# A graph layer on one Trainium2 core: grouped node sums from three bfloat16 parts instead of one float32 product

## The chip, the cores and the metric

The kernel runs on one core of one Trainium2 chip. The metric is the device time of one execution in microseconds (us). A core has a matrix engine (TensorE, shown as PE, with its weight loads shown apart as PEld), a vector engine (VectorE, DVE), a scalar engine (ScalarE, ACT), a general engine (GpSimd, POOL) and a queue for transfers (SyncE, SP). Each engine executes its own instructions in the order of the program, and the engines wait for one another by semaphores. Matmuls write to PSUM, which has eight banks here, split by the kernel into four with the tag "A" and four with the tag "B".

## The reference, cut to what matters

There are 6250 nodes with 128 features and 200,000 edges; `dst` is sorted, `src` is random. One layer computes

```python
h = relu(layernorm(x)); xw = h @ W_in                       # per node
W_ij = (shifted_softplus(f_ij @ W_f1 + b_f1) @ W_f2 + b_f2) * f_ij_cutoff   # per edge
x_ij = xw[idx_j] * W_ij
out  = segment_sum(x_ij, idx_i, num_segments=6250)          # idx_i = src, unsorted
y = x + shifted_softplus(out @ W_o1 + b_o1) @ W_o2 + b_o2
```

`idx_i` is `src` and `idx_j` is `dst`, so the gather follows the sorted index and the sum goes to random nodes. The sum over edges is the part that the change touches.

## The kernel before, in words

The edges are cut into 391 blocks of 512. `Plan` puts them in a list of 411 items, and one loop walks over it with a software pipeline: step `i` does the first stage of item `i`, the second of item `i-1` and so on. There are three kinds of items.

- **S items** (231): the product of an edge's filter and its gathered node row (`m`) goes through a matmul with an equality matrix (`s3_pe`, tile `pp`), is copied out by ScalarE (`s3_copy`, tile `s`), and is added to one of four accumulators in memory by four scatter transfers of 128 rows, issued by GpSimd (`scatter`, L491). Five buffers hold `s`.
- **B items** (160): the block's edges are first permuted by a matmul with a one-hot matrix (`perm_oh` makes it, `permute` writes the tiles `pf` and `po`, `perm_out` copies them out on ScalarE as `bfe` and `vf`), so that each edge lies in one of 512 places belonging to 16 groups of 392 nodes, 32 places each. Edges that find no place go to an overflow part, `po`. `b_ext` then multiplies by a small selection matrix to get each place's cutoff and its local node number; the result lies in 12 columns of the same bank as `po`, and `b_ext_copy` brings it to SBUF as `ex`. The product of filter and node row stays in SBUF as `bm`.
- **V items** (20): the overflow of eight B items, handled as an S item.

Eight B items are a **round**, 20 in all. When a round's eight products are there, four **units** sum them into `accT`, which holds all nodes in SBUF. Unit `s` of a round does for each of the eight blocks: a one-hot tile `so` of 128 places by 392 nodes, with the cutoff multiplied in (`unit_oh`, L671), and then per group of 32 places a matmul of the product by that one-hot tile (`unit_pe`, L686), 32 matmuls into four banks "B", one for each group. Being float32, each is two passes, so the profile counts 64. `unit_evac` (L694, L696) adds the four banks to `accT`.

The order of work is fixed by hand. Each step has named points, in order "L", "D0", the stages themselves, "A0", "A1", "DM", "PE2", "A2", "D2", and `at(step, point, function)` hangs work on them. A unit at step k has `unit_oh` at "D2" of step k-1, `unit_pe` at "PE2" of step k and `unit_evac` at "D1" of step k+1. A permutation planned for step u has `permute` at "PE2" of u, `perm_out` at "A0" of u+1, `b_ext` at "PE2" of u+1 and `b_ext_copy` at "D0" of u+2. `b_copy` brings a B item's gathered rows from PSUM to SBUF at "A0" of its own step.

The tiles with the tag "B" take the four banks in turn. A unit takes all four, so it waits for the readers of the four tiles that were taken before it. Most units come in pairs, at steps k and k+2 (32 times); the next one after a pair, or after a single unit, comes five or more steps later.

Plan lays a unit where the item two steps before is a B and the item after is an S. The products of B items, the index loads at the start and the loads of `x` for the tail share one pool `bp` of 16 buffers of 2 KB per partition.

After the loop, a tail sums the accumulators and `accT`, and computes the output layers.

Of the kernel before, what the change touches and what calls it, by code (L numbers as in the profile page):

```python
# [20 lines left out]
P = 128  # L21
# [29 lines left out]
def tile_gnn(ctx: ExitStack, tc: tile.TileContext, x, fS, fN, cT, srcT, srcr, dstr, dstT, base0, win_, wf1, wfB, wf2,  # L51
# [17 lines left out]
    NG = len(groups)  # L69
    XEARLY = min(8, len(tgroups))  # L70
    pl = Plan(NQ)
# [19 lines left out]
    dp = ctx.enter_context(tc.tile_pool(name="dp", bufs=1, space=DRAM))  # L91
    bp = ctx.enter_context(tc.tile_pool(name="bp", bufs=pl.nbm))
    edge = ctx.enter_context(ExitStack())
# [36 lines left out]
    iotw = cp.tile([P, GN // 2 + SLOTS], F16, name="iot")  # L130
    iot = iotw[:, GN // 2:]
    tri = cp.tile([P, P], BF16, name="tri")
    onesb = cp.tile([P, P], BF16, name="onesb")
# [278 lines left out]

    def b_copy(n):
        xc = wk.tile([P, 4, P], F32, tag="xc", name="xc")
        nc.scalar.copy(xc, bq[pl.items[n][1]].pop("xg"))
        st[n]["xc"] = xc

    def s2_m(n):
        kind, q = pl.items[n]
        if kind == "B":  # L420
            m = bp.tile([P, 4, P], F32, tag="bm", name="bm")
            bq[q]["m"] = m
        else:
            m = ms[pl.sd[n] % 2]
        nc.vector.tensor_tensor(m[:, :, :P], st[n]["W"], st[n]["xc"], op=ALU.mult)  # L425
        st[n]["m"] = m
        if kind == "B":
            del st[n]
# [198 lines left out]
    def perm_out(q):  # L627
        r, j = divmod(pl.bo[q], RND)
        f = wk.tile([P, 512], BF16, tag="bf", name="bfe", bufs=pl.nf)
        nc.scalar.copy(f[:KS], bq[q].pop("pf")[:KS])  # L630
        bq[q]["f"] = f
        if j == 0:
            vq[r] = {"f": wk.tile([P, 512], BF16, tag="vf", name="vf")}
        nc.scalar.copy(vq[r]["f"][:KS, j * OVC:(j + 1) * OVC], bq[q]["po"][:KS, :OVC])

# [4 lines left out]
    def b_ext(q):  # L640
        slot_ext(bq[q]["po"][:, OVC:OVC + 12], bq[q]["f"])

    def b_ext_copy(q):
        ex = wk.tile([P, 4, 3], F32, tag="ex", name="ex", bufs=pl.nex)
        nc.vector.tensor_copy(ex.rearrange("p c k -> p (c k)"), bq[q].pop("po")[:, OVC:OVC + 12])  # L645
        bq[q]["ex"] = ex
# [17 lines left out]

    so_t = {}

    def unit_oh(r, s):
        for q in pl.rounds[r]:
            so = wk.tile([P, GN], F32, tag="so", name="so", bufs=SOB)
            ex = bq[q]["ex"]  # L670
            nc.vector.tensor_scalar(so, iotw[:, :GN], ex[:, s, 1:2], ex[:, s, 0:1], op0=ALU.is_equal, op1=ALU.mult)  # L671
            so_t[q] = so

    un = {}

    def unit_pe(r, s):
        ts = []
# [3 lines left out]
        qs = pl.rounds[r]  # L681
        for q in qs:
            so = so_t.pop(q)
            for g in range(4):
                v = slice(g * CAP, (g + 1) * CAP)
                nc.tensor.matmul(ts[g][:, :GN], bq[q]["m"][v, s, :], so[v], start=(q == qs[0]), stop=(q == qs[-1]))  # L686
        un[r, s] = ts
# [22 lines left out]
    def x_load(g):  # L710
        o, T = tgroups[g]
        xts[g] = bp.tile([P, 4, P], F32, tag="bm", name="xb")
        nc.sync.dma_start(xts[g][:, :T], x[o:o + T * P, :].rearrange("(t p) f -> p t f", p=P))  # L713

    def load_idx(s, lo, hi):
        dst_sb = bp.tile([HALF, hi - lo], I32, tag="bm", name="dst_sb")
        nc.sync.dma_start(dst_sb, dstr[s * HALF:(s + 1) * HALF, lo:hi])
        src_i = bp.tile([HALF, hi - lo], I32, tag="bm", name="src_i")
        nc.sync.dma_start(src_i, srcr[s * HALF:(s + 1) * HALF, lo:hi])
        idx[s, lo] = (dst_sb, src_i)  # L720
# [7 lines left out]
    def src_cols(a, b):  # L728
        t_ = bp.tile([P, b - a], I32, tag="bm", name="srci")
        nc.sync.dma_start(t_, srcT[:, a:b])  # L730
        late["srci"] = t_
# [4 lines left out]
    def src_cast(s, lo, hi, eng):  # L736
        s16 = bp.tile([HALF, hi - lo], I16, tag="bm", name="s16")
        eng.tensor_copy(s16, idx[s, lo][1])
        nc.sync.dma_start(src16[s * HALF:(s + 1) * HALF, lo:hi], s16)

    with tc.manual_schedule():
# [56 lines left out]
        def rel(s, lo, hi):  # L798
            dst_sb = idx[s, lo][0]
            k0, k1 = lo // WSEG, hi // WSEG  # L800
            b_ = base_i[:, s, k0:k1]
            nc.vector.tensor_scalar(b_, dst_sb[:, ::WSEG], con[:HALF, 5 + s:6 + s], 0.0, op0=ALU.min, op1=ALU.max)
            rel_f = bp.tile([HALF, hi - lo], F32, tag="bm", name="rel_f")
# [3 lines left out]
            rel_b = bp.tile([HALF, hi - lo], BF16, tag="bm", name="rel_b")  # L807
# [56 lines left out]
        def at(i, point, fn, *a):  # L864
            hooks.setdefault((i, point), []).append((fn, a))
# [112 lines left out]
        for r, qs in enumerate(pl.rounds):  # L978
# [14 lines left out]
            for q in qs:  # L993
# [13 lines left out]
        for k, (r, s) in pl.units.items():  # L1007
# [3 lines left out]

        banked = {prep_tp: 1, prep_mm: 1, rank_count: 1, rank_over: 1, permute: 2, v_ext: 1, v_row: 1, late_bias: 1,
                  r0_tp: 1}
# [245 lines left out]
class Plan:  # L1259
    def __init__(self, nq):  # L1260
# [29 lines left out]
        for r, qs in enumerate(self.rounds):  # L1290
            i = max(self.pos[qs[-1]] + 2, done + 1)
            nxt = self.pos[self.rounds[r + 1][-1]] + 2 if r + 1 < len(self.rounds) else 0
            free = [k for k in range(i, nxt) if kind(k - 2) in ("B", "") and kind(k + 1) == "S" and kind(k) != "V"]
            rest = [k for k in range(max(free[-1:] + [i - 1]) + 1, i + 40) if "V" not in (kind(k), kind(k + 1))]
# [10 lines left out]
        self.perm, prev = {}, 0  # L1305
        for q in bs:
# [8 lines left out]
        self.nbm = 16  # L1315
        self.nf = 5
# [130 lines left out]
```

## Time and profile before

| | |
|---|---|
| three runs | 2489.48, 2496.16, 2496.21 us, median 2496.16 |
| the profiled execution | 2483.28 us |
| its span, first to last instruction | 2481.5 us |
| mean granted TensorE clock | 0.914 |
| busy: PE, DVE, ACT, POOL | 2074.5, 1723.3, 1528.0, 1648.4 us |
| units' matmuls (L686), busy | 621.1 us |
| units' one-hot tiles (L671), busy | 274.7 us |

Busy time is the union of an engine's instructions. A row of a group ends with the busy time, the mean of one instruction in ns, and the idle time of the engine just before those instructions, by what ended it. A wait between engines is given as the total, the number of times and the longest. In the timeline a row is a start, a length, the engine, the line and the instruction with its count, and in brackets the idle time before it and who ended it.

### The profile page before, as it was taken

To read this page: it belongs to the slowest core of one execution; us is meant where nothing else is said; L and a number is where in the kernel's file an instruction comes from. 1 tells how busy PE (TensorE), PEld (TensorE's weight loads), DVE (VectorE), ACT (ScalarE), POOL (GpSimd) and SP (SyncE) were. 2 spreads that over 40 slices of the span, in tenths; PEclk is the share of its full clock that TensorE was granted. 3 is DMA by queue.
4 is the path that set the end of the run, shared out by engine and by line. 5 is a ranking of instruction groups with operands and counts; after the bars stand their busy time and mean duration, and the time that the engine had idled before them with its cause. 6 is when DMAs were issued, how large, how long until landed. Compare 5 with 4: busy or idle time off the path is not lost. (4 is left out here: it accounts for less than half of the span.)

```text
span 2481.5 us, 50737 instructions
## 1 busy us (share of the span) xinstructions
PE 2074.5 (84%) x17477; PEld 1440.0 (58%) x17477; DVE 1723.3 (69%) x4345; ACT 1528.0 (62%) x3733; POOL 1648.4 (66%) x1060
## 2 busy tenths in 40 slices
PE   1678897988998898888889898989898897989955
PEld 1466665655665565655566565656566565656633
DVE  4666767677786767776776758677676766676744
ACT  1677565557575666656575765757576675667524
POOL 3578866748575667657585857677576776668674
PEclk8787898999998999989999999999999998999978
DMA  6766544536363455445464545455454554545748
GB/s 204 185 134 98 91 74 76 102 47 109 60 117 59 78 86 99 74 71 92 83 95 84 84 60 92 75 96 84 67 84 67 97 80 82 77 67 86 146 54 226
DMA packets 422469, 232.17 MB, mean 94 GB/s; under 512 B 156823, under 2 KB 399690, under 8 KB 422210
## 3 DMA queue, kind: packets, MB, share of 16 engines
q0 software_dynamic: 146032, 72.35, 28.7%
q1 hardware_dynamic: 275746, 156.49, 24.2%
q8 instruction: 138, 2.26, 0.4%
q14 instruction: 121, 0.99, 0.1%
q10 hardware_dynamic: 432, 0.08, 0.0%
HBM read 126.43 MB, written 102.32 MB: 92 GB/s over the span
## 5 line engine op out<-in xcount | busy, mean ns | idle before, releaser
L491 POOL DMA_INDIRECT acc<-s,ji x1003 | 1598.7, 1594 | 780.3 <-ACT ji L472 446.8
L686 PE MATMUL un<-so,bm 32*128 32x392 f32 x5120 | 621.1, 578 | 177.8 <-DVE ex L645 143.6
L447 ACT COPY s<-pp 128x258 f32<-128x258 f32 x502 | 172.8, 379 | 668.0 <-PE pp L439 485.4
L686 PEld LDWEIGHTS un<-so,bm 32*128 32x128 f32 x5120 | 332.0, 220 | 431.6 <-DVE ex L645 181.6
L401 PE MATMUL W<-w,a 128*128 128x128 f32 x3288 | 489.9, 293 | 3.5 <-DVE a L368 2.7
L401 PEld LDWEIGHTS W<-w,a 128*128 128x128 f32 x3288 | 410.2, 196 | 72.0 <-issue 32.1
L696 DVE TENSOR_TENSOR accT<-un,accT 128x392 f32<-128x392 f32 x304 | 150.8, 558 | 317.1 <-PE un L686 277.8
L368 DVE SCALAR_TENSOR_TENSOR a<-z,e 128x512 f32<-128x512 f32 x411 | 281.1, 684 | 110.3 <-ACT e L336 92.0
L439 PE MATMUL pp<-m,eq 128*128 128x129 f32 x2008 | 297.4, 291 | 12.4 <-DVE rt L601 4.9
L336 ACT ACTIVATE e<-e,con 128x512 f32<-128x512 f32 x411 | 296.7, 722 | 13.4
L439 PEld LDWEIGHTS pp<-m,eq 128*128 128x128 f32 x2008 | 267.5, 198 | 43.1 <-ACT s L447 6.5
L425 DVE TENSOR_TENSOR m<-W,xc 128x512 f32<-128x512 f32 x251 | 172.5, 687 | 168.9 <-ACT xc L410 148.4
L410 ACT ACTIVATE xc<-xg,cb 128x128 f32<-128x128 f32 x924 | 264.5, 380 | 25.3 <-PE xg L389 25.3
L330 ACT ACTIVATE e<-z 128x512 f32<-128x512 f32 x411 | 254.0, 618 | 39.5 <-PE z L315 21.9
L671 DVE TENSOR_SCALAR so<-iot,ex 128x392 f32<-128x392 f16 x640 | 274.7, 499 | 2.9 <-PE un L686 2.6
L331 ACT ACTIVATE e<-e 128x512 f32<-128x512 f32 x411 | 258.9, 630 | 13.1
L612 DVE TENSOR_SCALAR pm<-iot,pos 128x576 bf16<-128x576 f16 x640 | 205.3, 383 | 10.2 <-issue 6.8
L623 PE MATMUL pf<-pm,st 128*108 128x512 bf16 x640 | 203.5, 412 | 6.6 <-DVE ex L645 3.3
L384 PE MATMUL W<-b2rep,onesb 64*128 64x512 bf16 x411 | 161.9, 394 | 10.3 <-ACT xc L410 5.9
L307 PE MATMUL xgb<-wb,bfe 42*128 42x128 bf16 x1920 | 163.8, 220 | 0.0
L359 DVE TENSOR_TENSOR eq<-sb,srcT_sb 128x512 f32<-128x512 int16 x231 | 157.4, 682 | 1.3 <-issue 1.3
L304 PE MATMUL z<-bfe,wsb 64*128 64x512 bf16 (+2 forms) x480 | 152.0, 388 | 0.0
(171 smaller groups left out, 2217.1 us busy)
## 6 DMA issues: line engine op xcount, KB each, us to landing
sb<-src SPq DMA_DIRECT2D x231, 128.0 KB
acc<-s,ji POOLq DMA_INDIRECT x1003
rb<-reld SPq DMA_DIRECT2D x231, 64.0 KB
fsd<-f SPq DMA_DIRECT2D x29, 480.0 KB
ft<-fsd SPq DMA_DIRECT2D x115, 120.0 KB
fb<-in_fS_dram SPq DMA_DIRECT2D x29, 320.0 KB
ta_in<-acc SPq DMA_DIRECT2D x36, 256.0 KB
ft<-fsd SPq DMA_DIRECT2D x115, 80.0 KB
```

Of the source, the lines that this page charges most:

```text
L330: nc.scalar.activation(e, st[q]["z"], AF.Abs)
L331: nc.scalar.activation(e, e, AF.Exp, scale=-1.0)
L336: nc.scalar.activation(e, e, AF.Ln, bias=half, scale=0.5)
L368: nc.vector.scalar_tensor_tensor(a, st[q]["z"], 0.0, st[q]["l"], op0=ALU.max, op1=ALU.add)
L401: nc.tensor.matmul(W[:, c, :], st[n]["a"][:, c * P:(c + 1) * P], w2, start=False, stop=(c == 3))
L410: nc.scalar.mul(xc[:, c, :], st[n]["xg"][:, c, :], v)
L439: nc.tensor.matmul(pp[:, c, :129], st[n]["eq"][:, k, :], m[:, k, :129], start=True, stop=True)
L491: nc.gpsimd.indirect_dma_start(out=accs[k][:, :], out_offset=bass.IndirectOffsetOnAxis(ap=ji, axis=0), in_=s, in_offset=None, compute_op=A ...
L612: nc.vector.tensor_scalar(pm[:, c], iot[:, :SLOTS], rk[r]["pos"][:, 4 * j + c:4 * j + c + 1], None, op0=ALU.is_equal)
L623: nc.tensor.matmul(f[:KS], w, pm[:, c, :GRP * CAP], start=(c == 0), stop=(c == 3))
L671: nc.vector.tensor_scalar(so, iotw[:, :GN], ex[:, s, 1:2], ex[:, s, 0:1], op0=ALU.is_equal, op1=ALU.mult)
L686: nc.tensor.matmul(ts[g][:, :GN], bq[q]["m"][v, s, :], so[v], start=(q == qs[0]), stop=(q == qs[-1]))
```

## The change

The unit's matmuls become bfloat16. `unit_oh` splits the eight blocks' products for unit `s` into three bfloat16 parts: the high half of each float32 word, read in place as every second bfloat16 element (`high`), then the remainder's high half, then the rest (`low`). The one-hot tiles become bfloat16 and no longer carry the cutoff. `unit_pe` runs 96 single-pass matmuls, three per block and group, where it ran 64 passes. The cutoff is multiplied in earlier: `b_copy` becomes four ScalarE multiplications of 128 columns by `ex`, instead of one copy of 512.

`b_ext` now writes to a bank of its own, `be`, so `po` is done with when `perm_out` has copied it. `Plan.ext` puts `b_ext` at the first step after the permutation that is not a unit's; `b_ext_copy` follows one step later. The products lie in two fixed arrays of eight blocks, used by even and odd rounds, instead of the pool of 16, and the early temporaries and the loads of `x` use slices of them. Units have to lie two steps apart, which moves the last round's four from steps 405, 406, 407, 408 to 406, 408, 410, 412; all others stay. Ten permutations move later, by one or two steps.

```diff
@@ b_copy
-        nc.scalar.copy(xc, bq[pl.items[n][1]].pop("xg"))
+        xg = bq[q].pop("xg")
+        for c in range(4):
+            nc.scalar.mul(xc[:, c, :], xg[:, c, :], bq[q]["ex"][:, c, 0:1])
@@ s2_m
-            m = bp.tile([P, 4, P], F32, tag="bm", name="bm")
-            bq[q]["m"] = m
+            r, j = divmod(pl.bo[q], RND)
+            m = bms[r % 2][:, j]
@@ b_ext, b_ext_copy
-        slot_ext(bq[q]["po"][:, OVC:OVC + 12], bq[q]["f"])
+        t = ps.tile([P, 512], F32, tag="B", name="be", bufs=4)
+        slot_ext(t[:, :12], bq[q]["f"])
+        bq[q]["te"] = t
...
-        nc.vector.tensor_copy(ex.rearrange("p c k -> p (c k)"), bq[q].pop("po")[:, OVC:OVC + 12])
+        nc.vector.tensor_copy(ex.rearrange("p c k -> p (c k)"), bq[q].pop("te")[:, :12])
@@ unit_oh, unit_pe
+    def high(t):
+        return t.bitcast(BF16)[:, :, 1::2]
...
-        for q in pl.rounds[r]:
-            so = wk.tile([P, GN], F32, tag="so", name="so", bufs=SOB)
-            ex = bq[q]["ex"]
-            nc.vector.tensor_scalar(so, iotw[:, :GN], ex[:, s, 1:2], ex[:, s, 0:1], op0=ALU.is_equal, op1=ALU.mult)
+        m = bms[r % 2][:, :, s]
+        rm = wk.tile([P, RND, P], F32, tag="rem", name="rem", bufs=1)
+        nc.vector.tensor_tensor(rm, m, high(m), op=ALU.subtract)
+        lo = wk.tile([P, RND, P], BF16, tag="low", name="low", bufs=1)
+        nc.vector.tensor_tensor(lo, rm, high(rm), op=ALU.subtract)
+        for q in qs:
+            so = wk.tile([P, GN], BF16, tag="so", name="so", bufs=SOB)
+            nc.vector.tensor_scalar(so, iotw[:, :GN], bq[q]["ex"][:, s, 1:2], None, op0=ALU.is_equal)
...
-        for q in qs:
-            so = so_t.pop(q)
-            for g in range(4):
-                v = slice(g * CAP, (g + 1) * CAP)
-                nc.tensor.matmul(ts[g][:, :GN], bq[q]["m"][v, s, :], so[v], start=(q == qs[0]), stop=(q == qs[-1]))
+        for j in range(RND):
+            for k in range(3):
+                for g in range(4):
+                    v = slice(g * CAP, (g + 1) * CAP)
+                    nc.tensor.matmul(ts[g][:, :GN], parts[k][v, j, :], sos[j][v],
+                                     start=(j == 0 and k == 0), stop=(j == RND - 1 and k == 2))
@@ the schedule
-                at(u + 1, "PE2", b_ext, q)
-                at(u + 2, "D0", b_ext_copy, q)
+                at(pl.ext[q], "PE2", b_ext, q)
+                at(pl.ext[q] + 1, "D0", b_ext_copy, q)
@@ Plan
-            i = max(self.pos[qs[-1]] + 2, done + 1)
+            i = max(self.pos[qs[-1]] + 2, done + 2)
+            self.ext[q] = next(e for e in range(u + 1, p - 1) if e not in self.units)
+            load[self.ext[q]] = load.get(self.ext[q], 0) + 1
```

More of the change, by code (lines that the diff above doesn't have):

```diff
@@ L69, in tile_gnn @@
     NG = len(groups)
-    XEARLY = min(8, len(tgroups))
+    XEARLY = min(RND, len(tgroups))
     pl = Plan(NQ)
@@ L131, in tile_gnn, with tmp @@
     iot = iotw[:, GN // 2:]
+    bms = []
+    for i in range(2):
+        bm_ = cp.tile([P, RND, 4, P], F32, name=f"bm{i}")
+        bms.append(bm_)
+    tmp_n = [0]
+    def tmp(rows, n, dt):
+        k = tmp_n[0] % (2 * RND)
+        tmp_n[0] += 1
+        v = bms[k // RND][:rows, k % RND].rearrange("p s f -> p (s f)")
+        return v[:, :n] if dt == F32 else v.bitcast(dt)[:, :n]
     tri = cp.tile([P, P], BF16, name="tri")
@@ L413, in b_copy @@
     def b_copy(n):
+        q = pl.items[n][1]
         xc = wk.tile([P, 4, P], F32, tag="xc", name="xc")
-        nc.scalar.copy(xc, bq[pl.items[n][1]].pop("xg"))
+        xg = bq[q].pop("xg")
+        for c in range(4):
+            nc.scalar.mul(xc[:, c, :], xg[:, c, :], bq[q]["ex"][:, c, 0:1])
         st[n]["xc"] = xc
@@ L633, in perm_out @@
             vq[r] = {"f": wk.tile([P, 512], BF16, tag="vf", name="vf")}
-        nc.scalar.copy(vq[r]["f"][:KS, j * OVC:(j + 1) * OVC], bq[q]["po"][:KS, :OVC])
+        nc.scalar.copy(vq[r]["f"][:KS, j * OVC:(j + 1) * OVC], bq[q].pop("po")[:KS, :OVC])
     def slot_ext(t, f):
@@ L663, in v_row @@
         vq[r]["row"] = t
-    so_t = {}
+    def high(t):
+        return t.bitcast(BF16)[:, :, 1::2]
+    un = {}
     def unit_oh(r, s):
-        for q in pl.rounds[r]:
-            so = wk.tile([P, GN], F32, tag="so", name="so", bufs=SOB)
-            ex = bq[q]["ex"]
-            nc.vector.tensor_scalar(so, iotw[:, :GN], ex[:, s, 1:2], ex[:, s, 0:1], op0=ALU.is_equal, op1=ALU.mult)
-            so_t[q] = so
-    un = {}
+        qs = pl.rounds[r]
+        m = bms[r % 2][:, :, s]
[3 more added lines that the diff above has]
+        nc.vector.tensor_tensor(lo, rm, high(rm), op=ALU.subtract)
+        sos = []
+        for q in qs:
+            so = wk.tile([P, GN], BF16, tag="so", name="so", bufs=SOB)
+            nc.vector.tensor_scalar(so, iotw[:, :GN], bq[q]["ex"][:, s, 1:2], None, op0=ALU.is_equal)
+            sos.append(so)
+        un[r, s] = (high(m), high(rm), lo), sos
     def unit_pe(r, s):
+        parts, sos = un.pop((r, s))
         ts = []
@@ L1290, in __init__ @@
         for r, qs in enumerate(self.rounds):
-            i = max(self.pos[qs[-1]] + 2, done + 1)
+            i = max(self.pos[qs[-1]] + 2, done + 2)
             nxt = self.pos[self.rounds[r + 1][-1]] + 2 if r + 1 < len(self.rounds) else 0
             free = [k for k in range(i, nxt) if kind(k - 2) in ("B", "") and kind(k + 1) == "S" and kind(k) != "V"]
-            rest = [k for k in range(max(free[-1:] + [i - 1]) + 1, i + 40) if "V" not in (kind(k), kind(k + 1))]
+            rest = [k for k in range(max(free[-1:] + [i - 2]) + 2, i + 40, 2) if "V" not in (kind(k), kind(k + 1))]
             free = (free + rest)[:4]
@@ L1314, in __init__ @@
         self.nwin = 14
-        self.nbm = 16
         self.nf = 5
```

20 lines of the change are left out of this document (9 added, 11 removed).

## The prediction, made before the changed kernel ran

> **What bounds the kernel now.** I read the page's busy shares, then the waits, then the timeline around one pair of units. The page and its groups:
>
> ```profile
> span 2481.5 us, 50737 instructions
> ...
> PE 2074.5 (84%) x17477; PEld 1440.0 (58%) x17477; DVE 1723.3 (69%) x4345; ACT 1528.0 (62%) x3733; POOL 1648.4 (66%) x1060
> ...
> L491 POOL DMA_INDIRECT acc<-s,ji x1003 | 1598.7, 1594 | 780.3 <-ACT ji L472 446.8
> ...
> L686 PE MATMUL un<-so,bm 32*128 32x392 f32 x5120 | 621.1, 578 | 177.8 <-DVE ex L645 143.6
> ...
> L671 DVE TENSOR_SCALAR so<-iot,ex 128x392 f32<-128x392 f16 x640 | 274.7, 499 | 2.9 <-PE un L686 2.6
> ```
>
> The waits (total, times, longest):
>
> ```profile
> ACT s L447 <- PE pp L439: 485.4, 78, 14.2
> POOL acc L491 <- ACT ji L472: 446.8, 92, 36.2
> DVE accT L696 <- PE un L686: 277.8, 64, 7.6
> POOL acc L491 <- issue: 245.9, 805, 0.6
> ...
> DVE m L425 <- ACT xc L410: 148.4, 131, 19.2
> PE un L686 <- DVE ex L645: 143.6, 57, 6.2
> ...
> ACT s L447 <- DMA acc<-s,ji: 87.6, 19, 11.4
> ```
>
> No engine is full. The other engines wait for PE, and they do it at the units: ScalarE waits 485.4 us for matmuls that stand behind a unit, VectorE 277.8 us for the units' banks, and the scatter queue in turn 446.8 us for ScalarE. PE's own wait inside a unit is for `ex`. The chain that ended last is only the tail, so the timeline must show the price. A pair of units, steps 316 and 318, first VectorE, then PE, then ScalarE:
>
> ```profile
> 1859.90 3.23 DVE L671 TENSOR_SCALAR so<-iot,ex 128x392 f32<-128x392 f16 x8
> 1863.05 0.17 DVE L645 COPY ex<-po 128x12 f32<-128x12 f32 x1
> ...
> 1868.19 1.98 DVE L696 TENSOR_TENSOR accT<-un,accT 128x392 f32<-128x392 f32 x4 [1.74 <-PE un L686]
> ...
> 1871.29 3.23 DVE L671 TENSOR_SCALAR so<-iot,ex 128x392 f32<-128x392 f16 x8
> ...
> 1877.70 1.20 DVE L612 TENSOR_SCALAR pm<-iot,pos 128x576 bf16<-128x576 f16 x4
> 1878.82 0.16 DVE L645 COPY ex<-po 128x12 f32<-128x12 f32 x1
> ...
> 1885.60 1.99 DVE L696 TENSOR_TENSOR accT<-un,accT 128x392 f32<-128x392 f32 x4 [6.35 <-PE un L686]
> ...
> 1863.27 5.53 PE L686 MATMUL un<-so,bm 32*128 32x392 f32 x58 [1.68 <-DVE ex L645]
> ...
> 1875.94 0.24 PE L638 MATMUL po<-selb,bfe 108*128 108x3 bf16 x4 [0.77 <-ACT vf L634]
> 1876.11 0.93 PE L686 MATMUL un<-so,bm 32*128 32x392 f32 x6
> 1879.04 7.16 PE L686 MATMUL un<-so,bm 32*128 32x392 f32 x58 [2.00 <-DVE ex L645]
> ...
> 1875.66 0.22 ACT L634 CAST vf<-po 108x64 bf16<-108x64 f32 x1
> ```
>
> Both units stop after six passes, at the fourth bank, until an `ex` copy ends. The two are of different kinds. At the first, that copy stands directly behind the unit's own one-hot tiles: VectorE, without a gap, sets the start (1863.22, PE goes on at 1863.27). At the second, the fourth bank is the `po` permuted one step earlier. Its `ex` copy is planned for "D0" of the step after the unit, behind `pm`, so PE waits to 1879.04 though the tiles were ready at 1874.52. PE then runs slow (7.16 against 5.53 us), and VectorE, done at 1885.60 - 6.35 = 1879.25, idles 6.35 us.
>
> From the plan and the order in which the banks are taken, 37 of the 80 units have a permutation one step before (second kind), 38 are of the first kind, and five end the loop.
>
> **The change part by part.** *The second kind.* `po` is now free when ScalarE has copied `vf`. That copy moves later by the new `b_copy`, which stands before it at "A0":
>
> ```profile
> L415 ACT COPY xc<-xgb 128x512 f32<-128x512 f32 x160 | 92.2, 577 | 0.0
> ...
> L410 ACT ACTIVATE xc<-xg,cb 128x128 f32<-128x128 f32 x924 | 264.5, 380 | 25.3 <-PE xg L389 25.3
> ```
>
> One copy took 0.577 us; four multiplications take 264.5/231 = 1.145 us, so +0.57 us. The unit's length: each of 96 passes needs a weight load, and the row for four loads of 128 bfloat16 columns, beside rows for float32 loads and for a permutation's matmuls, is the first of these:
>
> ```profile
> 1875.83 0.26 PEld L638 LDWEIGHTS <-bfe 108*128 108x128 bf16 x4 [1.05 <-ACT bfe L630]
> ...
> 1879.85 0.35 PEld L686 LDWEIGHTS un<-so,bm 32*128 32x128 f32 x4 [0.30 <-issue]
> ...
> 1281.09 4.90 PEld L686 LDWEIGHTS un<-so,bm 32*128 32x128 f32 x58 [0.87 <-DVE ex L645]
> ...
> L638 PEld LDWEIGHTS <-bfe 108*128 108x128 bf16 x640 | 36.2, 97 | 58.2 <-ACT bfe L630 46.9 <-issue 4.6 <-ACT e L336 1.0
> ...
> 1217.37 0.40 PE L623 MATMUL pf<-pm,st 128*108 128x512 bf16 x1
> ...
> 1217.64 0.40 PE L623 MATMUL pf<-pm,st 128*108 128x512 bf16 x1
> ```
>
> (0.26 - 0.097)/3 = 0.054 us a load, 5.2 us a unit. The low end lets loads hide: a pass streams 576 columns (512 and po's 64) in 0.27 us, so 392 in 0.18, and four row groups run at once: 24 x 0.18 = 4.4 us. The high end takes the float32 load, (4.90 - 0.18)/57 = 0.083 us: 8.0 us. I take 5.2, since the loads have that row's width and type.
>
> [...] No row here shows a stepped load.
>
> At step 318 the unit ends at 1875.88 + 0.57 + 0.05 + 5.2 = 1881.7 instead of 1886.20: 4.5 us. VectorE must have finished its own work to profit; that slides by its extra 1.0 us (below), so at most 6.35 - 1.0 = 5.35 us comes through. The smaller of the two, unit by unit over the 37, sums to **199 us** (5.4 each; 188 to 207 for 1.5 and 0.6 us extra). First and last:
>
> ```profile
> 267.20 7.54 PE L686 MATMUL un<-so,bm 32*128 32x392 f32 x58 [4.37 <-DVE ex L645]
> ...
> 274.13 1.99 DVE L694 COPY accT<-un 128x392 f32<-128x392 f32 x4 [6.73 <-PE un L686]
> ...
> 2272.62 8.34 PE L686 MATMUL un<-so,bm 32*128 32x392 f32 x58 [2.21 <-DVE ex L645]
> ...
> 2280.35 1.98 DVE L696 TENSOR_TENSOR accT<-un,accT 128x392 f32<-128x392 f32 x4 [7.52 <-PE un L686]
> ```
>
> *VectorE's extra work.* Two subtractions over 8 x 128 elements. The neighbours:
>
> ```profile
> L254 DVE TENSOR_TENSOR fr<-fb,f 128x640 f32<-128x640 f32 x29 | 23.7, 817 | 0.0
> ...
> 1207.33 0.42 DVE L222 TENSOR_TENSOR rm<-xps,x 128x256 f32<-128x256 f32 x1
> ```
>
> 0.397 us for 384 elements more is 1.03 ns each, so 1.21 us for 1024, 2.4 for both. Eight bfloat16 tiles: `pm` does 576 columns in 1.20/4 = 0.30 us, the same operation with the same types; 392 columns lie between 0.20 (in proportion) and 0.30, and I take 0.25: 2.0 us. Together 4.4 against 274.7/80 = 3.4: **+1.0 us** a unit, ends +0.6 and +1.4.
>
> *The first kind.* The fourth bank is now mostly `be`, whose `ex` copy again stands directly behind `unit_oh`. These 38 units start 1.0 us later and take 5.2 instead of 5.53: +0.7. PE's wait grows from 1.68 to 2.7 us. The pair shows a slow unit after 2.00 us of waiting; I add 0.4, since some of the 38 are slow already (ends 0 and 1.5, the excess of 7.16 over 5.53 in proportion). 38 x 1.1 = **-42 us**, ends +20 (a unit of 4.4 us, +0.6) and -98.
>
> [...]
>
> *ScalarE.* 160 x 0.57 = 91 us. Six of a round's eight B items stand around units, where ScalarE idles for `pp` (485.4 us) and the `vf` part is already counted. Two stand between, where VectorE waits on ScalarE (148.4 us for `xc`): 40 x 0.57 = **-23 us**, ends 0 and -91. If the idle time goes, all 91 are paid.
>
> *The rest.* `ex` copies stay 160; `be` adds one bank taken per B item, but `po` leaves earlier, so I cost it at nothing; what covers it is the VectorE order, and without that a wait of `pp` for an `ex` copy is next. The last units spaced by two let the scatter queue fill: **+6 us**, ends 0 and 10. Fixed arrays keep the rotation of 16 products; nothing. The scatters do not change: 1003 x 1.594 + 245.9 = 1845 us, below the forecast. DMAs and SP's queue keep their number and place, except as steps move.
>
> Sum: 199 - 42 - 23 + 6 = 140 us. Against the profiled execution's 2483.28 that is 2343; the median of the runs, 2496.16, lies 12.9 us above it, so **2356 us**.
>
> **The rivals.**
>
> *Stepped weight loads cost like float32* (slower). A unit takes 8.0 us. On PE's side alone the second kind saves 5.9 us on average (4.5 at step 318), now 5.9 - 2.8 = 3.1, or 115 us, which VectorE no longer limits; the first loses 1.0 + 2.5 + 0.4 = 3.9, or 148; ScalarE 23, the last five 4: 2483 + 60, or about 2556 with the same offset. It decides from 7.3 us a unit, 0.076 a load. For it: no stepped load is in the trace. Against: a float32 load reads every byte that a stepped one spans, and in the row of four the next loads follow at (0.35 - 0.18)/3 = 0.055 us, as the bfloat16 loads do.
>
> *VectorE and ScalarE take all of it* (no change). All ends at once: 188 - 98 - 91 = -1, so 2497. For it: VectorE then has no gap between a pair's units. Against: three ends must meet.
>
> *The scatter queue gives part back.* The 87.6 us in which ScalarE waits for a free `s` grow when PE is sooner. If half the gain goes there, 2426. Against: the queue starves 446.8 us, and starvation is what shrinks.
>
> *More comes out.* The low unit length, no ScalarE cost: 207 + 20 + 6 = 233, so 2263.
>
> **How the numbers follow.** Forecast (2310 to 2410) 0.56; scatter queue 0.15; more 0.11; no change 0.08, of which 0.05 within bounds and 0.03 slower; stepped loads 0.10. Faster: 0.56 + 0.15 + 0.11 = 0.82. Three runs spread by 0.3%, which is what a measurement can tell. The range 2265 to 2475 leaves out the no-change and stepped-load cases above, 0.18, and the edge of the case below.
>
> **What would show it.** Right: L686's successor shows no wait on `ex` at the second kind but one on `vf` of about 1.3 us, 5.2 us from its fourth bank to its end, and its busy time falls from 621.1 to some 430; VectorE's wait for `un` falls from 277.8 to under 120; the scatter queue's for `ji` from 446.8 to about 310; the first kind still waits for `ex`, longer. Wrong: weight loads spaced over 0.07 us, or waits of PE on the new `low` and `so` tiles.

## The result, and the profile after

The changed kernel takes **2306.96 us** (median of four runs, 2301.08 to 2313.85) against 2495.05 (2489.48 to 2496.21), a ratio of 0.9251 with a 95% interval of 0.9222 to 0.9281. Profiled execution against profiled execution it is 2307.47 against 2483.28: **176 us less**, where the sum of the prediction gave 140; by the medians it is 188. The time lies inside the range of 2265 to 2475, 49 us below the point.

In this kernel's profile the unit's matmul is L709, its one-hot tiles L695, the two subtractions L689 and L691, the multiplied `b_copy` L428, `ex`'s copy L660, the sum into `accT` L720, `b_ext`'s matmuls L651. From its page:

```profile
span 2305.3 us, 56334 instructions
PE 1915.0 (83%) x20037; PEld 1376.3 (60%) x20037; DVE 1793.0 (78%) x4505; ACT 1613.1 (70%) x4213; POOL 1675.5 (73%) x1060
```

From its groups by line:

```profile
L504 POOL DMA_INDIRECT acc<-s,ji x1003 | 1625.8, 1621 | 576.5 <-ACT ji L485 249.9 <-issue 233.2 <-DMA acc<-s,ji 52.2
L709 PE MATMUL un<-so,bm 32*128 32x392 bf16 x2560 | 378.7, 377 | 181.5 <-DVE so L695 79.9 <-DVE ex L660 43.1 <-ACT xc L428 22.3
L695 DVE TENSOR_SCALAR so<-iot,ex 128x392 bf16<-128x392 f16 x640 | 162.0, 326 | 0.0
L691 DVE TENSOR_TENSOR low<-rem 128x1024 bf16<-128x1024 f32 x80 | 98.0, 1225 | 2.7
L689 DVE TENSOR_TENSOR rem<-bm 128x1024 f32<-128x1024 f32 x80 | 97.5, 1219 | 0.0
L428 ACT ACTIVATE xc<-xgb,ex 128x128 f32<-128x128 f32 x640 | 181.8, 370 | 0.0
L651 PE MATMUL be<-selb,bfe 108*128 108x3 bf16 x640 | 39.8, 166 | 8.9 <-ACT bfe L643 7.1 <-DVE rt L614 0.7 <-issue 0.4
```

From its waits (total, times, longest):

```profile
POOL acc L504 <- ACT ji L485: 249.9, 76, 35.7
ACT s L460 <- PE pp L452: 238.8, 65, 8.0
DVE accT L720 <- PE un L709: 138.7, 60, 5.5
PEld L709 <- DVE so L695: 126.9, 75, 4.9
PE un L709 <- DVE so L695: 79.9, 43, 4.5
ACT s L460 <- DMA acc<-s,ji: 76.7, 18, 8.4
PE un L709 <- DVE ex L660: 43.1, 31, 1.7
```

The three large waits of before have halved or nearly: ScalarE for `pp` 485.4 to 238.8, the scatter queue for `ji` 446.8 to 249.9, VectorE for the units' banks 277.8 to 138.7. What has grown is PE's wait for one-hot tiles, from 18.7 us to 79.9 (its weight loads, which come first, show 126.9). The wait for `ex` inside a unit has fallen from 143.6 to 43.1 and no longer occurs at the second kind.

The same pair of units as in the prediction, steps 316 (first kind) and 318 (second), in the timeline; first VectorE, then PE:

```profile
1716.73 1.23 DVE L691 TENSOR_TENSOR low<-rem 128x1024 bf16<-128x1024 f32 x1
...
1717.87 1.98 DVE L695 TENSOR_SCALAR so<-iot,ex 128x392 bf16<-128x392 f16 x8
1719.78 0.16 DVE L660 COPY ex<-be 128x12 f32<-128x12 f32 x1
...
1725.51 1.99 DVE L720 TENSOR_TENSOR accT<-un,accT 128x392 f32<-128x392 f32 x4 [2.53 <-PE un L709]
...
1728.61 1.22 DVE L689 TENSOR_TENSOR rem<-bm 128x1024 f32<-128x1024 f32 x1
1729.86 1.22 DVE L691 TENSOR_TENSOR low<-rem 128x1024 bf16<-128x1024 f32 x1
1731.00 1.94 DVE L695 TENSOR_SCALAR so<-iot,ex 128x392 bf16<-128x392 f16 x8
...
1737.88 1.99 DVE L720 TENSOR_TENSOR accT<-un,accT 128x392 f32<-128x392 f32 x4 [1.48 <-PE un L709]
...
1718.24 0.34 PE L709 MATMUL un<-so,bm 32*128 32x392 bf16 x3 [1.95 <-DVE so L695]
...
1719.99 0.48 PE L709 MATMUL un<-so,bm 32*128 32x392 bf16 x1 [1.40 <-DVE ex L660]
...
1720.29 0.83 PE L709 MATMUL un<-so,low 32*128 32x392 bf16 x4
...
1720.62 0.83 PE L709 MATMUL un<-so,bm 32*128 32x392 bf16 x4
...
1723.18 0.48 PE L709 MATMUL un<-so,bm 32*128 32x392 bf16 x4
...
1723.35 0.48 PE L709 MATMUL un<-so,rem 32*128 32x392 bf16 x4
...
1731.78 0.34 PE L709 MATMUL un<-so,bm 32*128 32x392 bf16 x1
1732.58 0.32 PE L709 MATMUL un<-so,bm 32*128 32x392 bf16 x1 [0.46 <-ACT xc L428]
1733.06 0.43 PE L709 MATMUL un<-so,bm 32*128 32x392 bf16 x2 [0.15 <-ACT bfe L643]
1733.18 0.48 PE L709 MATMUL un<-so,rem 32*128 32x392 bf16 x4
...
1736.84 0.47 PE L709 MATMUL un<-so,low 32*128 32x392 bf16 x4
```

At step 318 the unit stops for 0.46 and 0.15 us in ScalarE's order (`b_copy`, then `bfe` and `vf`), and from 1733.06 it runs through: four passes each 0.166 us, 22 such rows in the 3.66 us from 1733.18 to 1736.84. VectorE idles 1.48 us before it, where it idled 6.35. At step 316 PE waits 1.95 us for the first one-hot tile, does three passes, stops 1.40 us at the fourth bank for the `ex` copy behind the eighth tile, and then needs 0.33 us for four passes until about 1722.3, and 0.17 after. The granted clock is 1.00 up to the first passes there and 0.50 from 1720 to 1722.3.

All 80 units, sorted by the kind that they had in the kernel before (37 of the second kind, 38 of the first, and the five that end the loop). The numbers are means per unit, worked out from each unit's rows; "PE" is the wait before its first pass plus the time from there to the end of its last:

| kind | PE, before | PE, after | wait before the first pass | wait for `ex` inside | VectorE idle before `accT` |
|---|---|---|---|---|---|
| second (37) | 11.94 | 6.12 | 0.00 to 0.64 | 3.33 to 0.00 | 6.67 to 0.56 |
| first (38) | 8.36 | 9.49 | 0.44 to 1.88 | 0.54 to 1.13 | 2.18 to 2.62 |
| last five | 7.90 | 8.68 | 0.41 to 0.92 | 0.00 to 0.00 | 1.42 to 4.44 |

That is 37 x 5.82 = 215 us gained, 38 x 1.13 = 43 lost and 5 x 0.78 = 4 lost: 168 of the 176. The other 8 are a gain and a loss elsewhere. The gain is at `b_ext`'s matmuls. The group of before, not shown in the prediction:

```profile
L638 PE MATMUL po<-selb,bfe 108*128 108x3 bf16 x640 | 39.4, 166 | 35.1 <-ACT vf L634 34.3 <-issue 0.8
```

Before, they stood one step behind the permutation, directly ahead of a unit where that step had one, and PE idled 35.1 us, nearly all for ScalarE's copies of the permuted tiles; now, at a step without a unit, 8.9: 26 us gained in this accounting, which goes by PE's time; no run moves `b_ext` alone. What is left, 176 - 168 - 26 = -18 us, is the loss in all other places.

### The profile page after: what moved, and what is told of

The parts are those of the page before. It is cut to its first block, busy times and chain, and to the rows that moved or that the text cites. A ratio compares the mean times of both kernels' runs of the same rounds, so it can differ in the third digit from the quotient of the medians.

```text
span 2305.3 us, 56334 instructions
## 1 busy us (share of the span) xinstructions
PE 1915.0 (83%) x20037; PEld 1376.3 (60%) x20037; DVE 1793.0 (78%) x4505; ACT 1613.1 (70%) x4213; POOL 1675.5 (73%) x1060
## 3 DMA queue, kind: packets, MB, share of 16 engines
q14 instruction: 125, 1.02, 0.1%
## 4 chain that ended last, share of the span: by engine, by line
DVE 27%; PE 26%; ACT 20%; issue 8%; DMA 7%; POOL 6%; SPq 5%; ACTq 0%; DVEq 0%; POOLq 0%
PE un L709 14%; DMA acc<-s,ji 6%; POOL acc L504 5%; DVE so L695 4%; PE W L411 4%; ACT xc L420 4%; ACT xc L428 3%; ACT e L341 3%; DVE a L378 3%; ACT e L340 3%; PE pp L452 3%; DVE accT L720 3%; DVE rem L689 3%; ACT s L460 2%; DVE bm L438 2%
## 5 line engine op out<-in xcount | busy, mean ns | idle before, releaser
L504 POOL DMA_INDIRECT acc<-s,ji x1003 | 1625.8, 1621 | 576.5 <-ACT ji L485 249.9
L709 PE MATMUL un<-so,bm 32*128 32x392 bf16 x2560 | 378.7, 377 | 181.5 <-DVE so L695 79.9
L460 ACT COPY s<-pp 128x258 f32<-128x258 f32 x502 | 172.0, 385 | 365.8 <-PE pp L452 238.8
L709 PE MATMUL un<-so,rem 32*128 32x392 bf16 x2560 | 352.4, 379 | 0.0
L709 PE MATMUL un<-so,low 32*128 32x392 bf16 x2560 | 349.3, 375 | 0.0
L452 PEld LDWEIGHTS pp<-m,eq 128*128 128x128 f32 x2008 | 265.3, 197 | 64.0 <-ACT s L460 12.9
L720 DVE TENSOR_TENSOR accT<-un,accT 128x392 f32<-128x392 f32 x304 | 150.8, 558 | 139.8 <-PE un L709 138.7
L709 PEld LDWEIGHTS <-bm 32*128 32x128 bf16 x2560 | 139.0, 106 | 196.3 <-DVE so L695 126.9
L709 PEld LDWEIGHTS <-rem 32*128 32x128 bf16 x2560 | 132.7, 106 | 115.4 <-issue 81.8
L428 ACT ACTIVATE xc<-xgb,ex 128x128 f32<-128x128 f32 x640 | 181.8, 370 | 0.0
```

Of the source, the lines that this page charges most:

```text
L428: nc.scalar.mul(xc[:, c, :], xg[:, c, :], bq[q]["ex"][:, c, 0:1])
L452: nc.tensor.matmul(pp[:, c, :129], st[n]["eq"][:, k, :], m[:, k, :129], start=True, stop=True)
L504: nc.gpsimd.indirect_dma_start(out=accs[k][:, :], out_offset=bass.IndirectOffsetOnAxis(ap=ji, axis=0), in_=s, in_offset=None, compute_op=A ...
L709: nc.tensor.matmul(ts[g][:, :GN], parts[k][v, j, :], sos[j][v], start=(j == 0 and k == 0), stop=(j == RND - 1 and k == 2))
L720: nc.vector.tensor_tensor(v, t[:, :GN], v, op=ALU.add)
```

## The experiments

Each is a version of one of the two kernels. Ratios are to the kernel before, which was measured again beside each group of versions, with medians of 2490.49, 2492.68 and 2494.95 us. A difference of some 5 us between versions of different groups therefore says little.

| version | median us (range) | ratio [95%] |
|---|---|---|
| before, bank alone | 2248.86 (2247.14 to 2250.91) | 0.9031 [0.9014, 0.9049] |
| after, bank undone | 2539.59 (2537.51 to 2543.51) | 1.0200 [1.0179, 1.0222] |
| after, cutoff left out | 2251.76 (2243.55 to 2256.61) | 0.9044 [0.9013, 0.9074] |
| after, no subtractions | 2153.88 (2149.64 to 2161.14) | 0.8655 [0.8629, 0.8681] |
| the same, one part | 2113.97 (2109.22 to 2118.63) | 0.8466 [0.8445, 0.8488] |
| before, bank and cutoff | 2268.60 (2266.32 to 2271.37) | 0.9092 [0.9070, 0.9115] |
| after, early `ex` | 2241.59 (2236.60 to 2243.88) | 0.8978 [0.8954, 0.9002] |
| before, bank and early `ex` | **2198.12** (2195.90 to 2204.27) | 0.8818 [0.8795, 0.8842] |
| after, tiles first | 2304.08 (2299.28 to 2310.32) | 0.9235 [0.9216, 0.9254] |
| after, early `ex`, tiles first | 2217.71 (2212.99 to 2222.51) | 0.8901 [0.8884, 0.8919] |
| after, early `ex`, cutoff left out | 2203.84 (2199.48 to 2208.43) | 0.8838 [0.8817, 0.8859] |

**Which part of the change gains?** The theory was the prediction's: the bank does, and the split alone loses or breaks even. The rival was that cheaper matmuls carry it. First the bank and its schedule alone, with float32 units:

```diff
-        slot_ext(bq[q]["po"][:, OVC:OVC + 12], bq[q]["f"])
+        t = ps.tile([P, 512], F32, tag="B", name="be", bufs=4)
+        slot_ext(t[:, :12], bq[q]["f"])
...
-                at(u + 1, "PE2", b_ext, q)
-                at(u + 2, "D0", b_ext_copy, q)
+                at(pl.ext[q], "PE2", b_ext, q)
+                at(pl.ext[q] + 1, "D0", b_ext_copy, q)
...
```

> The kernel before, with the bank part alone: the product for cutoff and place gets a bank of its own at the new steps, and the units stay float32 with the cutoff in the one-hot tiles. Theory of the prediction (the wait for the ex copy at the fourth bank is the gain): the 37 units of the second kind start when ScalarE has copied vf, without the 0.57 us of the new multiplications, and take 5.5 us; each saves about 6.0 us, the first kind is as before, so 222 us less than 2495, about 2275 (2255 to 2305), which would be faster than the whole change. Rival (the shorter bfloat16 unit is the gain): at most 60 us less, 2435 or more.

Then the changed kernel with this part undone:

> The changed kernel, with the bank part undone: the product for cutoff and place goes back into po's bank at the old steps, and the units stay three bfloat16 parts, the cutoff on ScalarE. Theory: the second kind still waits for the late ex copy, 1.0 us later than before, and is 1.5 us shorter (18 us saved), the first kind starts 1.0 us later and is about 1.4 us shorter (15 us saved), ScalarE costs 23: within 25 us of before, 2470 to 2520. Rival (the shorter unit is the gain): 2400 or less.

Measured 2248.86 and 2539.59. The waits of the bank alone (the unit's matmul is L688 there), and then its groups by line:

```profile
ACT s L447 <- PE pp L439: 265.3, 62, 8.3
DVE accT L698 <- PE un L688: 101.9, 47, 4.7
PE un L688 <- DVE ex L647: 14.9, 16, 1.8
```

```profile
L688 PE MATMUL un<-so,bm 32*128 32x392 f32 x5120 | 560.5, 525 | 48.0 <-DVE so L673 16.5 <-DVE ex L647 14.9 <-issue 5.7
...
L638 PE MATMUL be<-selb,bfe 108*128 108x3 bf16 x640 | 39.8, 166 | 6.5 <-ACT bfe L630 4.7 <-DVE ra L600 0.6 <-issue 0.6
```

The same two views of the kernel with the bank undone:

```profile
PE un L707 <- DVE ex L658: 202.8, 70, 7.1
DVE accT L718 <- PE un L707: 327.5, 74, 6.8
```

```profile
L651 PE MATMUL po<-selb,bfe 108*128 108x3 bf16 x640 | 39.4, 166 | 62.6 <-ACT vf L647 58.7 <-ACT xc L428 2.6 <-ACT bfe L643 1.3
```

The bank gains 246 us without the split (2495 to 2249, or 242 against the kernel before of its own group) and 233 with it (2540 to 2307); the split loses 45 without the bank and 58 with it. So the bank is more than the whole gain. The same float32 unit that took 11.94 us takes 6.36 at the second kind when nothing stops it. Of these 5.6 us, 3.5 are waits, and 2.1 are busy time (8.45 to 6.36): before, the mean granted clock inside these units was 0.78, and below 0.9 in 36 of the 37; with the bank alone it is 1.00 in all of them. Weighted by the granted clock the busy time hardly changes (6.50 to 6.36), so the slow clock after the stop is this second part of the price. The run lies below the theory's range, which began at 2255: beside the units, `b_ext`'s own wait fell from 35.1 us to 6.5. The part as a whole was tested; no run separates the bank of its own from the moved step of `b_ext` and the ten moved permutations.

With the bank undone the units wait 202.8 us in all for `ex`, 158 of them at the second kind, where it was 123 before, since `ex` now stands behind more VectorE work. And `b_ext` waits 62.6 us for ScalarE where it waited 35.1, since the four multiplications stand ahead of the copies that it reads. The theory's range ended at 2520; this second loss was not in it.

**What does the cutoff cost?** First it is taken out of the changed kernel, by the edit below. Then the multiplications are put into the version with the bank and float32 units, by the reverse of this edit; the one-hot tiles there no longer multiply by the cutoff.

```diff
-        for c in range(4):
-            nc.scalar.mul(xc[:, c, :], xg[:, c, :], bq[q]["ex"][:, c, 0:1])
+        nc.scalar.copy(xc, xg)
```

> The changed kernel, with one ScalarE copy of 512 columns in place of the four multiplications; the cutoff is left out for the blocks of the grouped sums. Theory: the multiplications cost 23 us, so 2284 (2275 to 2300). Rival (ScalarE sets the stretches between the units): all 91 us come back, 2216.

> The bank part alone, and the cutoff multiplied on ScalarE as in the change, the units still float32 (one-hot tiles without the cutoff, 64 passes). Theory (ScalarE's 91 us come through by the 55 that leaving them out gave): 2249 + 55 = 2304, or up to 20 less if the one-hot tile with one operation is quicker than 0.43 us: 2280 to 2310. It would put nearly the whole loss of the split against the bank alone on ScalarE. Rival (the subtractions, +1.0 us of VectorE a unit, are the loss): 2249 to 2265.

Measured: 55 us less (2307 to 2252), and 20 us more (2249 to 2269). A third run, below, gives 38. ScalarE's work is the same each time, 181.8 us in the changed kernel against 92.2 before, so in the changed kernel and its version with the early copy two to three fifths of the 90 us come through. The 20 us of the float32 version is a net figure: its one-hot tiles became cheaper, 232.9 us of VectorE against 277.1 with the bank alone, and how much of that offsets the multiplications was not measured. Neither expectation holds for both: in the changed kernel the cost lies between theory and rival, in the float32 version just above the rival's range.

**What do the subtractions cost?** The two are left out, and the high part is used three times:

```diff
-        rm = wk.tile([P, RND, P], F32, tag="rem", name="rem", bufs=1)
-        nc.vector.tensor_tensor(rm, m, high(m), op=ALU.subtract)
-        lo = wk.tile([P, RND, P], BF16, tag="low", name="low", bufs=1)
-        nc.vector.tensor_tensor(lo, rm, high(rm), op=ALU.subtract)
...
-        un[r, s] = (high(m), high(rm), lo), sos
+        un[r, s] = (high(m), high(m), high(m)), sos
```

> The changed kernel, without the two subtractions per unit: the high part is used for all three, so the lower parts of the products are left out; 96 matmuls as before. Theory (VectorE sets the start of the first kind, and the second is covered): 38 units start up to 2.4 us sooner, 60 to 93 us less, 2214 to 2247. Rival (VectorE's extra work is covered everywhere): within 10 us of 2307. Rival (VectorE binds both kinds): 150 us or more less, under 2160.

153 us less (2307 to 2154), of 195.5 us of VectorE work (97.5 + 98.0): the rival's number. By the units' rows, the first kind's 9.49 us fall to 6.28, 122 us over 38 units, the second kind's 6.12 to 5.46, 24 us, and the last five's 8.68 to 5.36, 17 us. Together that is 163, ten more than the whole. So it is mainly the first kind and the end of the loop that pay for VectorE's work. The first kind pays 3.2 us a unit for 2.4 us of subtractions; inside these units the mean granted clock rises from 0.75 to 0.93 without them.

Then one part instead of three, 32 passes a unit:

```diff
-            for k in range(3):
+            for k in range(1):
...
```

> The changed kernel without subtractions and with one of the three matmul parts, so 32 passes a unit; the lower parts of the products are left out. Against the run without subtractions (2154), PE has 2.8 us less a unit, 222 us in all. Theory (without the subtractions PE is again what a unit waits for): half or more comes through, 2000 to 2050. Rival (VectorE and ScalarE hold it): 2120 or more. The scatters alone need 1845 us.

40 us less (2154 to 2114), near the rival's 2120 and far from the theory's 2000 to 2050. The units' PE time falls by 2.93 and 2.58 us at the two kinds and grows by 1.85 at the last five, 37 x 2.93 + 38 x 2.58 - 9 = 197 us, and four fifths of that do not reach the end. Without the subtractions PE's passes are not what bounds most of the loop.

**Is the first kind's loss at its fourth bank?** There the `ex` copy stands behind the whole of `unit_oh`. Moving it ahead, to the "D2" of the step before when the next step is a unit:

```diff
-                at(pl.ext[q] + 1, "D0", b_ext_copy, q)
+                if pl.ext[q] + 1 in units:
+                    at(pl.ext[q], "D2", b_ext_copy, q)
+                else:
+                    at(pl.ext[q] + 1, "D0", b_ext_copy, q)
```

> The changed kernel, with the ex copy ahead of the unit's subtractions and one-hot tiles where a unit follows the step of the product (end of that step instead of the start of the next). Theory (the wait of the first kind at the fourth bank, 43 us on ex, is on the path, behind the wait for the one-hot tiles): 25 to 45 us less, 2262 to 2282. Rival (the one-hot tiles hold it anyway): within 10 us of 2307.

> The bank part alone, with the ex copy ahead of the unit's one-hot tiles. Waits for ex at the units are 14.9 us there: theory 10 to 20 us less, 2229 to 2239. Rival (VectorE's order is what it needs, and the copy moved forward holds up the one-hot tiles): 2249 to 2265.

65 us less than the changed kernel, 51 less than the bank alone: both more than the waits for `ex` on PE, 43.1 and 14.9 us, on which the expectations stood. The waits of the first; then the waits and the units' group of the second:

```profile
PE un L709 <- DVE so L695: 98.9, 52, 4.5
DVE accT L720 <- PE un L709: 70.6, 40, 5.5
```

```profile
ACT s L447 <- PE pp L439: 183.6, 53, 7.1
DVE accT L698 <- PE un L688: 57.9, 31, 4.7
```

```profile
L688 PE MATMUL un<-so,bm 32*128 32x392 f32 x5120 | 525.8, 516 | 33.5 <-DVE so L673 14.6 <-DVE rm L222 10.3 <-DVE pr L577 3.3
```

Here a stop cost more than its own length. After the early copy VectorE's wait for the units' banks is 70.6 us in the changed kernel (138.7 without it) and 57.9 in the float32 version (101.9). In the float32 version the units' matmuls are busy 525.8 us instead of 560.5, with the same 5120 instructions: 35 us less, on top of the 15 us of waiting, together nearly the 51. These 35 us come from the first kind's units, whose busy time falls from 7.64 to 6.63 us each. The slow clock is only a part of that: weighted by the granted clock the fall is still 6.78 to 6.09. So about a third is the clock, and where the rest comes from stays open. The mean clock of whole executions does not show it (0.947 to 0.955 with the bank alone, 0.947 to 0.958 with the early copy). In the changed kernel the first kind falls from 9.49 to 7.57 us, 73 us in all, and the second grows by 0.20, 7 us: 66, against 65 measured; the units of the first kind with a granted clock below 0.9 go from 33 to 20. The version with the bank and the early copy, and without the split, is the fastest at **2198 us**; the split costs 44 us there.

**Is it the place of the subtractions, or their time?** PE waits for the one-hot tiles because the subtractions stand ahead of them. Turned round, and the passes part by part:

```diff
-        rm = wk.tile([P, RND, P], F32, tag="rem", name="rem", bufs=1)
...
         for q in qs:
...
             sos.append(so)
+        rm = wk.tile([P, RND, P], F32, tag="rem", name="rem", bufs=1)
...
-        for j in range(RND):
-            for k in range(3):
+        for k in range(3):
+            for j in range(RND):
```

> The changed kernel with the eight one-hot tiles made ahead of the two subtractions, and the unit's passes ordered part by part (all eight blocks' high halves first, then the middle parts, then the low ones). VectorE does the same work. Theory (what is lost is the start: PE waits for the one-hot tiles 79.9 us at 43 units, of which the subtractions are 2.4 us each): a unit of the second kind starts 2.4 us sooner and ends about 0.9 sooner, since VectorE gives the low part 4.4 us after its start and 32 passes of 4.16/96 us follow; the first kind still stops at its fourth bank until the ex copy behind all of the unit's VectorE work, so it gains nothing and waits longer. 2307 less 20 to 40: 2267 to 2287. Rival (VectorE's time counts wherever it stands, as its removal without any other change gave 153 of 195 us): within 0.5 per cent of 2307, 2296 to 2318.

> The same edit on the version with the early ex copy, so that the fourth bank holds up neither kind. There PE waits for the one-hot tiles 98.9 us, 52 times. Theory (the start is what is lost): 52 units end 0.9 us sooner, 47 us, and fewer of them run in the slow clock: 2242 less 35 to 60, 2182 to 2207. Rival (VectorE's time counts wherever it stands): 2230 to 2250.

Waits of the first, and then of the second:

```profile
DVE accT L720 <- PE un L709: 128.0, 54, 6.8
PE un L709 <- DVE ex L660: 74.7, 35, 3.7
PE un L709 <- DVE so L691: 11.8, 6, 2.3
```

```profile
DVE accT L720 <- PE un L709: 31.9, 17, 5.2
PE pp L452 <- DVE accT L720: 16.9, 17, 2.7
PE un L709 <- DVE so L691: 14.8, 12, 2.1
```

In the changed kernel it gives nothing (2307 to 2304): the wait for one-hot tiles falls from 79.9 to 11.8, and the wait for `ex` grows from 43.1 to 74.7, with the first kind at 9.60 us where it was 9.49. With the early copy it gives 24 us, less than the 35 to 60 of the theory. There the units do become shorter, by 1.02 us at the first kind, 0.37 at the second and 0.37 at the last five, 55 us in all; but PE now waits longer at the next matmuls for VectorE to empty the banks (16.9 us, 5.4 without the new order), and of the 55 less than half reach the end. So the place is a part of it. That the time on VectorE is the larger part is argued from the 153 us above; the subtractions were not left out of the version with the early copy.

Last, the cutoff taken out of the version with the early copy (the edit is the one above):

> The version with the early ex copy, with b_copy as one plain copy (the cutoff is left out of the grouped sums, so that the output lacks that factor). The four multiplications cost 55 us in the changed kernel (2307 to 2252) and 20 us in the version with float32 units (2249 to 2269). Theory (the 55 holds some 35 us of one more thing, the wait of b_copy and of what stands behind it for an ex copy that comes late behind the unit's VectorE work; the early copy takes it away): 2242 less 15 to 30, 2212 to 2227. Rival (with VectorE near its limit the 91 us of ScalarE count at full rate in every version with the split): 2242 less 45 to 65, 2177 to 2197.

38 us (2242 to 2204), between the two again. The late `ex` copy can account for some 17 of the 55; that ScalarE's work counts at a full rate is not so either. What sets the share was not settled.

## Why the prediction was right, and where it was off

The outcome and the mechanism hold; by the terms of the sum, in the order of the prediction:

| term | predicted | from the rows of the two profiles |
|---|---|---|
| second kind | 199 | 215 |
| first kind | -42 | -43 |
| `b_ext`'s own wait | costed at nothing | 26 |
| last five units | 6 | -4 |
| ScalarE and all else | -23 | -18 (what is left) |
| sum | 140 | 176 |

**The second kind** lost its wait for `ex` altogether, as forecast. The forecast of 1.3 us of waiting on ScalarE's `vf` was too high: at step 318 the waits for ScalarE are 0.46 + 0.15. Over the 37 units they come to 12.7 us, and waits for VectorE to 25.6 (16.5 for one-hot tiles, 9.1 for the ranking's `pr`). The unit was mis-sized. Spaced by weight loads at 0.054 us it would take 5.2; it takes 4.16 where nothing stops it (the second unit of the loop, from 266.77 to 270.93), with four passes each 0.166 us. The loads are busy for 2.42 us of these 4.16, while passes run, and the four groups do run at once: their passes start within 0.01 us of one another, and one takes 0.324 us (median). So the low end of the bounds was the nearest, and even that (4.4) was above it. The second kind's average stays near the forecast all the same, 5.48 us from first pass to last end, since many units carry short waits or run slow for a part (5 have a mean granted clock below 0.9); that the two agree is luck.

**The stepped load**, the rival that would have made the kernel slower, is refuted. Four passes, each with a load of its own, come each 0.166 us, so 0.042 us a load, where the rival decided from 0.076. And the median of one load (shortest, median and longest in ns behind the count) is the same for the high halves with a step of two as for the contiguous `low`; the float32 loads of before had 185.

```profile
L709 PEld LDWEIGHTS <-bm x2560: 91/93/147, 253.1 to 2229.5; 32*128 32x128 bf16 x197
L709 PEld LDWEIGHTS <-low x2560: 90/93/147, 254.1 to 2229.8; 32*128 32x128 bf16 x197
```

So the step of two costs nothing here: 93 ns with it and 93 without.

That rival's saving of 5.9 us a unit on PE's side alone comes to 6.3 from the rows of the 37 units, which would have put it near 2540 instead of 2556; nothing else rests on it.

**VectorE's extra work** was sized right: 97.5 + 98.0 + 162.0 = 357.5 us against 274.7, 1.03 us a unit for a forecast of 1.0.

**The first kind** came out as summed, -43 for -42, but not as worked out. The forecast had PE wait 2.7 us at the fourth bank. In the trace the wait is split: 1.88 us before the first pass, since the subtractions also stand ahead of the first one-hot tile, and 1.13 at the fourth bank. That the sum agrees is luck, since two errors cancel. All waits of such a unit grew by 2.1 us (0.44 + 0.74 to 1.88 + 1.42) for 1.0 in the forecast. The busy time of the passes fell by 1.0 (7.18 to 6.18), where the forecast had 5.2 for 5.53 and 0.4 more for the slow clock. The slow clock was mis-sized most: 4.16 us where nothing stops the unit, 6.18 here, with the granted clock below 0.9 in 33 of the 38 units (9 before).

**`b_ext`'s own wait** is the term that was put at nothing and was not. The change part costed the rest of the bank's edit at nothing and looked only at who takes the banks and when they are left. `Plan.ext` also moves the matmul itself off a place where PE stood waiting for ScalarE just ahead of a unit. The row for it, 0.77 us before the unit of step 318, stands in the prediction's own timeline, and was read for the unit's weight loads only. By the accounting this is 26 of the 36 us by which the sum fell short.

**The last five** lost instead of gaining: VectorE idles 4.44 us before the `accT` sums of each, and PE takes 8.68 us for each. Without the subtractions it takes 5.36.

**ScalarE** is not a term that can be given one size: what is left over in the accounting is -18, while taking the multiplications out gives 55 in the changed kernel. Part of that stands inside the units' rows (PE waits for `xc` in units), which are 19 + 14 + 1 = 34 us shorter without the multiplications, and so in the first two lines of the table.

**The offset**: 12.9 us were added for the median above the profiled execution; after the change the two agree within 0.5 us (2306.96 and 2307.47). This is the rest of the 49 us: 36 + 13. It belongs to the executions and not to the change: the profiled one of before, 2483.28, is quicker than all four others (2489.48 to 2496.21).

Of the signs named, the busy time of the unit's matmuls was to be some 430, and is 448.6 us (the number behind the comma, from the view of busy time by window, taken over the whole span):

```profile
0.00:2305.30 2305.30, 448.61 (x7680) 273.67 (x7680) 0.92 0.59 101
```

The scatter queue's wait for `ji` fell below the forecast of 310, to 249.9, as the gain was larger. VectorE's wait for `un` was to be under 120 and is 138.7: the first kind and the last five hold 38 x 2.62 + 5 x 4.44 = 122 of it. The rival by which the scatter queue gives part back did not occur: ScalarE's wait for a free `s` fell from 87.6 to 76.7. Waits of PE on the new tiles, named as a sign against, are there, 79.9 us, of which 58.9 stand at the first kind; they did not make the sum wrong, and they are where the first kind went another way than forecast. That the split as such gains nothing was implied by the terms and not said: the forecast's 199 joined the bank and the faster unit, and the runs separate them, 246 for the bank alone and -58 for the split on top of it.

## What to carry to other kernels

Before an expensive rewrite of a matmul, look at why it stops: here one bank, shared by two results with different readers, held 37 units for 3.3 us each and left their passes at a mean granted clock of 0.78, and the part that gave it up gained more than the whole change (246 us against 188). A new operation on the engine that feeds a stage is paid at the instances where that engine already comes last (here 3.2 us a unit at the first kind and 0.7 at the second, for 2.4 us of subtractions), so count those instances apart from the others. When a result is moved to another step, look up the wait of the moved instruction itself, not only those of its readers (here 35.1 us before and 8.9 after).

## What the runs showed of the hardware

**Here the slow clock followed short waits.** At step 316, after 1.95 and 1.40 us of waiting with three passes between, the granted clock is 0.50 and four passes take 0.33 us for some 2.3 us, and then 0.17. In the kernel before, one wait of 2.00 us behind six passes was followed by a granted clock of 0.50 from 1879 to 1882 us (step 318). The passes follow the clock by the same factor: four take 0.33 us at 0.50 and 0.166 at 1.00.

**Scatters that overlapped a subtraction took longer.** The mean scatter is 1621 ns in the changed kernel, 1594 before, and 1592 without the subtractions:

```profile
L504 POOL DMA_INDIRECT acc<-s,ji x1003 | 1596.6, 1592 | 450.3 <-issue 229.0 <-ACT ji L485 112.9 <-DMA acc<-s,ji 65.2
```

By their rows in the changed kernel, the 82 scatters that overlap the first subtraction by over 0.3 us take 1905 ns on average and the 70 that overlap the second 2095, against 1597 and 1585 for those that do not touch it. Overlap as such did not lengthen a scatter here: with the `accT` sums, which read one input from PSUM, it is 1546 against 1633. With the equality matrices, which read both from SBUF, it is 1659 against 1618, a much weaker effect. Both inputs of these subtractions lie in SBUF too. What makes the scatters longer was not tested. The rise from 1594 to 1621 ns is 27 us over 1003 scatters, on a queue that still starves for 249.9 us, so probably a small part of the subtractions' cost; how much of the 153 us it is was not measured.

**The one-operation one-hot tile was cheaper with bfloat16 output**: the same single comparison on the same float16 input took 432 ns with float32 output in the version with bank and cutoff (L676, 232.9 us for 640), and 326 in the changed kernel with bfloat16 output (162.0 us for 640).
